# A pre-norm transformer block on one core: the value operands' differences moved into their pair's own iteration, and the background rounding at the end of attention queued behind norms and copies

## The chip, the cores and the metric

The kernel runs on 1 core of one Trainium2 chip. The metric is the device time of one execution in microseconds; before the change it is 2465.94 us, the median of 3 runs (2464.23 to 2466.81). Five engines work side by side, each in the order of its own instruction list: TensorE (PE, matmuls and transpositions through the array), VectorE (DVE), ScalarE (ACT), GpSimd (POOL) and SyncE (SP, which here only issues DMAs). They wait for each other through semaphores.

## The reference

One block with a residual stream of 2048 tokens by 1024 channels, all in float32:

```
x = x + attention(layernorm(x))       # per token: 32 heads of 32 attend to each other
x = x + w3' (silu(w1' xn) * (w2' xn)) # xn = layernorm(x), hidden size 2752
```

Attention is unusual: for each token, the 32 heads' queries (32 x 32) are multiplied with the 32 heads' keys of the same token, a softmax runs over the 32 head scores, and the result weighs the 32 heads' values. So it is 2048 little 32x32 problems, and no token sees another one. The three projections have biases. A fourth projection of the reference ("latent") isn't used for the output.

w1', w2' and w3' are the weights rounded to a 16-level code and back: each block of 64 weights is divided by its largest magnitude, every quotient goes to the nearest of 16 fixed levels, and the result is multiplied by the magnitude again. The kernel must do this rounding itself, with the inputs given in full precision.

## The kernel before

**Products.** Every large product is done by a Strassen-Winograd scheme: operands are cut into four quarters, a few sums and differences of quarters (the names S1 to S4 for the left operand, T1 to T4 for the right one) are made first, and seven products of quarters replace eight. `three`, `fourth` and `differences` (L419 to L430) make S1 to S4 of a token pair's operand with four VectorE operations L420, L421, L422 and L425 of 128x512 each.

**Stages.** Tokens are handled in 16 tiles of 128, in 8 pairs. There are four stages:

1. Query sweep, one iteration per pair (p = 0 to 7). VectorE normalizes the two tiles (L358 writes xn), TensorE transposes xn (L517), four blocks of 512 columns for a pair, and ScalarE copies each block out of PSUM twice: into the operand A in token order (L520) and into the operand V in another token order (L522). The third block's copies go to A21 and V21. PSUM has three buffers `pt` for these blocks. `products` (L373 to L417) multiplies A with the query weights; its helper calls `fill(n)` after some products, and there other work is put in: background turns, and at n = 5 the transpositions of the next pair (`nxt.transposes`). After the products, `nxt.finished()` makes the next pair's A differences and writes A to DRAM (opD), `now.finished_v()` makes the current pair's V differences and writes V (opV). A has two buffers, V, A21 and V21 have one each. `qk_T` turns the query product and stores it; `weight_chunk` makes T1 to T4 of a slice of the key or value weights.
2. Key sweep: A comes back from DRAM, is multiplied with the key weights, and `scores` and `softmax_T` do the 32x32 score problems.
3. Value sweep: V comes back from DRAM and is multiplied with the value weights. `gather` does the 32x32 products of probabilities and values, half a tile per `part()` call, into the one PSUM buffer `at`. After the second half `residual` (L722 to L732) transposes `at` into the tile cx on VectorE (L725), adds it to the tile x1 of the block's input (L729), writes the sum to DRAM (x1d, L731, two DMAs of 128x512) and normalizes it (L358 through `normed`). `keep_T` transposes the normed tile on TensorE (L768), copies it out on ScalarE (L769), makes T1 to T4 on VectorE (L784, tiles xU) and writes all to DRAM.
4. Feed-forward. Weight units of 128 hidden channels (`Unit`, seven products per unit) and then the down projection in groups (`down7`, and `down` at the end). Between the third and the fourth stage, `plain_block` multiplies the first unit (chunk 0) without the seven-product scheme while the last four tiles' `part()` calls and `keep_T` calls are threaded through its steps (L908 to L934).

**The background.** `background` is a generator that rounds the FFN weights, chunk after chunk. One `next` is a turn. A turn is one rounding step: either one VectorE operation (L257, L259, L261), or a ScalarE activation (L266 into a tile sg, two buffers) followed by a VectorE operation (L267); some turns also hold the block maxima (`absmax`, L230 to L238) or the scaling (`scaled`, sixteen ScalarE operations of 128x64 at L218, or one VectorE operation at L214). `advance(n)` takes n turns; `flush` does the transpositions and copies (L178, L179) of a finished chunk. In the feed-forward stage turns are paced by TensorE's time (`spent`).

**What sets the order.** TensorE's instructions are issued as written (`manual_schedule`). For the other engines and the DMA issues a list scheduler sets the order at compile time, from the order in which the program traces them, their dependences and its own estimate of durations; it also hands out the buffers. Three devices steer it. `tc.issue_after(ins)` queues what is traced in the block behind `ins` on `ins`'s engine. `marked(ins)` remembers a ScalarE copy, and where `urgent["rule"]` names "scale" or "step", the background's ScalarE work is queued behind the last remembered copy (`behind`). `held["behind"]`, if set, queues whole background turns behind one VectorE instruction (`turn`); `hook["normed"]` is the newest norm (L358).

Of the kernel before, what the change touches and what calls it, by code (L numbers as in the profile page):

```python
# [14 lines left out]
ALU = mybir.AluOpType  # L15
# [16 lines left out]
TB = 512  # L32
# [37 lines left out]
def preln_block_kernel(  # L70
# [14 lines left out]
    nc = tc.nc  # L85
# [38 lines left out]
    held = {"behind": None}  # L124
# [155 lines left out]
    def advance(n):  # L280
        for _ in range(n):
            with turn():
                next(bg, None)
# [22 lines left out]
    NP = NT // 2  # L306
# [43 lines left out]
    def normed(src, dst, order=None):  # L350
        mv = small.tile([P, 2], FP, tag="mv", name="mv")
        rs = small.tile([P, 1], FP, tag="rs", name="rs")
        mean_var(small, src, mv)
        with tc.issue_after(order["last"]) if order else nullcontext():
            order_end = inv_std(rs, mv[:, 1:2])
        if order is not None:
            order["last"] = order_end.ins
        done = nc.vector.tensor_scalar(dst, src, mv[:, 0:1], rs, ALU.subtract, ALU.mult)  # L358
        hook["normed"] = done.ins
        return dst  # L360
# [185 lines left out]
    nxt = Inputs(0)  # L546
# [25 lines left out]
    opened = last.ins  # L572
# [24 lines left out]
    for p in range(NP):  # L597
        more = p + 1 < NP
        now = nxt
        urgent["rule"] = ("scale",) if p == 0 else ()  # L600
        if more:
            load_x(2 * p + 2)
            load_x(2 * p + 3)
            with nullcontext() if p else tc.issue_after(opened):
                nxt = Inputs(p + 1)
            if p == 0:
                with tc.issue_after(hook["normed"]):
                    nc.vector.tensor_tensor(W["T4"], W["B21"], W["T2"], ALU.subtract)

        def fill(n):  # L610
            if n in (7, 3):
                flush(1)
            if n == 5 and more:
                nxt.transposes(0)
                nxt.transposes(1)
            with nullcontext() if p else tc.issue_after(opened):
                advance({3: 3, 4: 2}.get(n, 0) if p == 0 else int(n != 5))

        cs = products(now.A, fill, (lambda name: None) if more else next_W("k"), ps_t)
        flush(1)  # L620
        if more:
            nxt.finished()
        for j in range(2):
            t = work.tile([P, 32, NH], FP, tag="qd", name="qd", bufs=2)
            qk_T(t, cs[j], qb_sb)
            nc.sync.dma_start(qD[2 * p + j], t)
        with nullcontext() if p else tc.issue_after(opened):
            now.finished_v()
        weight_chunk("kv"[p // 4], p % 4)
        advance(2)  # L630
        if p == NP - 2:
            first = load_A(opD, 0)
# [89 lines left out]
    def residual(i, at, x1):  # L722

        cx = work.tile([P, E], FP, tag="cx", name="cx")
        nc.vector.transpose(  # L725
            cx.rearrange("p (h d) -> p d h", d=D),
            at[:, :, 0:256].rearrange("p c (s d) -> p d s c", d=D),
        )
        nc.vector.tensor_tensor(x1, x1, cx, ALU.add)  # L729
        for n in range(2):  # L730
            nc.sync.dma_start(x1d[i][n], x1[:, ts(n, TB)])  # L731
        return normed(x1, x1)  # L732

    ops = {}

# [51 lines left out]
    for p in range(NP):  # L787
        if p + 1 < NP:
            nextA = load_A(opV, p + 1)
        else:  # L790

            until("2", 0)
            nextA = work.tile([P, 4, 4, P], FP, tag="w0", name="w0")
            nc.sync.dma_start(nextA, wd["2", 0][:, 0:4])
        i = 2 * p - 4

        def fill(n):
            if n in (7, 2, 5, 4) and (p, n) != (1, 7):
                part()
            advance({7: 2, 6: 2, 5: 1, 3: 2}.get(n, 0))  # L800
            if n in (7, 4):
                flush(1)
            if n == 5 and i in x1n:
                keep_T(i, x1n.pop(i))
            if n == 3:
                if p == 0:
                    part()
                elif i + 1 in x1n:
                    keep_T(i + 1, x1n.pop(i + 1))

        cs = products(A, fill, (lambda name: None) if p + 1 < NP else next_op)
        flush(1)
        if p == 0:
            sweep.close()
            sweep = ExitStack()
            work = sweep.enter_context(
                tc.tile_pool(name="workv", bufs=1, side="right", reuse_waits="tile")
            )
        pl = load_tiles(pD, p, "pl", 3)
        for j in range(2):  # L820
            t = work.tile([P, 32, D], FP, tag="vd", name="vd", bufs=3)
            v_T(t, cs[j], vb_sb)
            parts.append(gather(2 * p + j, pl[j], t))
        advance(2)
        A = nextA
    hook["scale"] = "both"
    urgent["rule"] = ()
    left.close()


# [74 lines left out]

    plain = plain_block(A, 0)  # L908
    i = NT - 4
    next(plain)  # L910
    next(plain)
    part()
    advance(1)
    next(plain)
    keep_T(i, x1n.pop(i))
    part()
    advance(2)
    flush()
    next(plain)
    part()  # L920
    advance(2)
    next(plain)
    keep_T(i + 1, x1n.pop(i + 1))
    part()
    advance(3)
    next(plain)
    part()
    advance(3)
    next(plain)
    keep_T(i + 2, x1n.pop(i + 2))  # L930
    hs = {0: next(plain)}
    advance(3)
    held["behind"] = hook["normed"]
    keep_T(i + 3, x1n.pop(i + 3))  # L934
    sweep.close()
    sweep_at.close()
# [20 lines left out]
    class Unit:  # L957
# [13 lines left out]
        def first(self):  # L971
            self.z = ps_z.tile([P, TB], FP, tag="z", name="z")
            self.mul(1, self.z, True, False)
            self.g0 = hp.tile([P, TB], FP, tag="g0", name="g0", bufs=2)
            nc.scalar.copy(self.g0, self.z)  # L975

        def middle(self):
            q = self.q = ps_q.tile([P, TB], FP, tag="q", name="q")
            self.mul(7, q, True, False)
            self.mul(6, self.z, False, False)  # L980
            u2 = self.u2 = hp.tile([P, TB], FP, tag="u2", name="u2")
            nc.scalar.copy(u2, self.z)
            r = ps_r.tile([P, TB], FP, tag="r", name="rr")
            self.mul(2, r, True, True)
            nc.vector.tensor_tensor(self.g0, self.g0, r, ALU.add)  # L985
            nc.scalar.activation(self.g0, self.g0, AF.Silu)
            self.mul(5, self.z, False, False)
            u4 = hp.tile([P, TB], FP, tag="u4", name="u4")
            nc.scalar.copy(u4, self.z)  # L989
            self.h = [new_h(), new_h()]  # L990
            nc.vector.tensor_tensor(self.h[1], u4, q, ALU.add)

# [195 lines left out]
    for n, (g, tbp) in enumerate(passes):  # L1188
        half, sides = None, []
        while now is not None and now.tbp == tbp and now.c in g:  # L1190
            unit = now
            unit.middle()
            if unit.c == min(g[-1], NFULL - 1):
                for c in [c for c in w3T if c not in g]:
                    del w3T[c]
                ask_w3(g)
            if g[-1] == NFULL and unit.c == NFULL - 1:
                half = Half(tbp)
                half.part(0)
                hs[unit.c] = unit.last()  # L1200
                half.part(1)
                hs[NFULL] = half.h
                now = None
            if units:
                now = Unit(*units.pop(0))
                now.first()
            if unit.c < PAIRED and unit.c % 2:
                side = Sides(hs[unit.c - 1], n == 0, len(sides))
                hs[unit.c] = unit.last(side.second)
                sides.append(side.both(hs[unit.c][0]))  # L1210
            elif half is None:
# [46 lines left out]
```

## Time and profile before

| | |
|---|---|
| median of 3 runs | 2465.94 us |
| lowest and highest | 2464.23, 2466.81 us |
| profiled execution, its own time | 2468.05 us |
| its span, first to last instruction | 2466.3 us |
| granted TensorE clock, mean | 0.989 |
| PE, DVE, ACT, POOL busy | 2384.2, 2015.7, 1514.9, 290.0 us |
| DMA | 513.87 MB, mean 208 GB/s |

Busy times are those of instructions of each engine; an engine that waits, or whose sequencer only issues DMAs, counts as idle. In a timeline row the columns are start, length, engine, line, operation, output and inputs by the program's tile names, and the count of merged instructions; a bracket holds the idle time of that engine just before the row, and which engine's instruction ended it. TensorE rows of eight matmuls are one product of the seven (four matmuls of 128x512 in the program, two rows for each in the profile). The stages lie at about 0 to 262 us (queries), 262 to 510 us (keys), 510 to 762 us (values), 762 to 816 us (plain block with the last four tiles), and the rest is the feed-forward.

### The profile page before, as it was taken

To read this page: it belongs to the slowest core of one execution; us is meant where nothing else is said; L and a number is where in the kernel's file an instruction comes from. 1 tells how busy PE (TensorE), PEld (TensorE's weight loads), DVE (VectorE), ACT (ScalarE), POOL (GpSimd) and SP (SyncE) were. 2 spreads that over 40 slices of the span, in tenths; PEclk is the share of its full clock that TensorE was granted. 3 is DMA by queue.
4 is the path that set the end of the run, shared out by engine and by line. 5 is a ranking of instruction groups with operands and counts; after the bars stand their busy time and mean duration, and the time that the engine had idled before them with its cause. 6 is when DMAs were issued, how large, how long until landed. Compare 5 with 4: busy or idle time off the path is not lost.

```text
span 2466.3 us, 36345 instructions
## 1 busy us (share of the span) xinstructions
PE 2384.2 (97%) x14000; PEld 1114.6 (45%) x14000; DVE 2015.7 (82%) x2239; ACT 1514.9 (61%) x2819; POOL 290.0 (12%) x364
## 2 busy tenths in 40 slices
PE   8899999999998899999999999999999999999998
PEld 4444455545554344444444444444444444444433
DVE  8999888679899789898989989899898998861022
ACT  4556644134445678778787786977878778751200
POOL 1010000001001012030030301203012030020300
PEclk9999999999998999999999999999999999999999
DMA  8788643656779577485784858848588385772983
GB/s 320 279 298 351 237 161 115 230 204 224 231 247 317 192 261 164 141 177 187 280 178 141 177 172 298 171 147 182 163 294 194 125 187 160 276 167 78 179 317 113
DMA packets 179549, 513.87 MB, mean 208 GB/s; under 512 B 15984, under 2 KB 70256, under 8 KB 156976
## 3 DMA queue, kind: packets, MB, share of 16 engines
q1 hardware_dynamic: 138672, 438.08, 48.7%
q0 software_dynamic: 40704, 73.47, 18.2%
q8 instruction: 110, 1.80, 0.3%
q14 instruction: 63, 0.52, 0.1%
HBM read 283.69 MB, written 227.80 MB: 207 GB/s over the span
## 4 chain that ended last, share of the span: by engine, by line
DVE 23%; issue 21%; PE 14%; ACT 7%; DMA 3%; POOL 1%; DVEq 0%; POOLq 0%; ACTq 0%; SPq 0%
DVE r L267 15%; PE z L364 5%; DMA x1d<-acc 3%; PE z L1070 2%; ACT sg L266 2%; PE q L364 2%; ACT wn L218 2%; PE po L1151 1%; ACT r L218 1%; PE y L1070 1%; DVE r L259 1%; DVE r L261 1%; ACT acc L1083 1%; DVE am L230 1%; PE rr L364 1%
## 5 line engine op out<-in xcount | busy, mean ns | idle before, releaser
L267 DVE SCALAR_TENSOR_TENSOR r<-sg,r 128x1024 f32<-128x1024 f32 x780 | 946.8, 1214 | 84.8 <-ACT sg L266 51.6
L266 ACT ACTIVATE sg<-wn 128x1024 f32<-128x1024 f32 x780 | 815.1, 1054 | 305.9 <-DVE r L267 280.6
L1085 POOL DMA_DIRECT2D x1d<-acc x280 | 244.2, 926 | 1281.0 <-ACT acc L1083 1238.1
L364 PE MATMUL z<-xB,w 128*128 128x512 f32 x720 | 327.1, 602 | 5.9 <-ACT u L989 4.2
L364 PE MATMUL z<-xT,w 128*128 128x512 f32 x656 | 300.5, 601 | 11.7 <-ACT g L975 8.0
L364 PE MATMUL q<-xT,w 128*128 128x512 f32 x656 | 291.3, 592 | 0.0
L1070 PE MATMUL z<-w,h 128*128 128x512 f32 x496 | 230.8, 593 | 2.9 <-ACT acc L1083 2.9
L364 PEld LDWEIGHTS z<-xB,w 128*128 128x128 f32 x720 | 135.1, 193 | 170.2 <-issue 152.9
L364 PEld LDWEIGHTS z<-xT,w 128*128 128x128 f32 x656 | 123.2, 192 | 165.7 <-issue 139.5
L218 ACT ACTIVATE wn<-wn,rc 128x64 f32<-128x64 f32 x736 | 189.3, 341 | 8.9 <-DVE rc L238 8.9
L364 PEld LDWEIGHTS q<-xT,w 128*128 128x128 f32 x656 | 123.2, 190 | 148.6 <-issue 146.4
L364 PE MATMUL z<-wT,A 128*128 128x512 f32 x384 | 177.1, 604 | 0.1
L364 PE MATMUL q<-wT,A 128*128 128x512 f32 x384 | 172.8, 592 | 0.0
L1070 PE MATMUL y<-w,h 128*128 128x512 f32 x320 | 152.0, 596 | 3.6 <-DVE h L1048 3.1
L364 PE MATMUL z<-wB,A 128*128 128x512 f32 x320 | 148.5, 608 | 2.0 <-ACT u L383 2.0
L364 PE MATMUL rr<-xB,w 128*128 128x512 f32 x328 | 147.5, 592 | 0.0
L1070 PEld LDWEIGHTS z<-w,h 128*128 128x128 f32 x496 | 92.6, 190 | 116.9 <-issue 100.8
L218 ACT ACTIVATE r<-r,am 128x64 f32<-128x64 f32 x456 | 116.6, 344 | 16.1 <-DVE r L267 16.0
L1083 ACT COPY acc<-z 128x512 f32<-128x512 f32 x160 | 92.6, 585 | 38.0 <-PE z L1070 29.7
L364 PEld LDWEIGHTS q<-wT,A 128*128 128x128 f32 x384 | 72.1, 190 | 86.7 <-issue 84.9
L985 DVE TENSOR_TENSOR g<-g,rr 128x512 f32<-128x512 f32 x41 | 28.0, 682 | 100.7 <-PE rr L364 100.7
L137 POOL TENSOR_TENSOR rs<-mv,eps 128x1 f32<-128x1 f32 x32 | 18.0, 562 | 762.5 <-DVE mv L134 762.5
(136 smaller groups left out, 2733.6 us busy)
## 6 DMA issues: line engine op xcount, KB each, us to landing
x1d<-acc POOLq DMA_DIRECT2D x280, 256.0 KB, 6.5
wd<-wop SPq DMA_DIRECT2D x31, 2048.0 KB, 7.3
w<-wd SPq DMA_DIRECT2D x41, 1280.0 KB, 7.7
wn<-in_w_dram SPq DMA_DIRECT2D x63, 512.0 KB, 4.2
xT<-xdT SPq DMA_DIRECT2D x28, 1024.0 KB, 8.5
xB<-xdB SPq DMA_DIRECT2D x24, 1024.0 KB, 7.0
w<-wd SPq DMA_DIRECT2D x42, 512.0 KB, 4.4
w<-wd SPq DMA_DIRECT2D x10, 1536.0 KB, 7.6
```

The lines of the kernel that those rows point to most:

```text
L218: nc.scalar.mul(dst[:, ts(n, BLOCK)], src[:, ts(n, BLOCK)], by[:, n : n + 1])
L230: nc.vector.tensor_reduce(am[:, :nb], v.rearrange("p (b e) -> p b e", e=BLOCK), AX.X, ALU.max, apply_absolute_value=True,)
L259: nc.vector.scalar_tensor_tensor(r, v, edge, r, ALU.is_lt, ALU.max)
L261: nc.vector.scalar_tensor_tensor(r, v, edge, r, ALU.is_gt, ALU.subtract)
L266: nc.scalar.activation(t, v, AF.Copy, bias=-edge * by, scale=by)
L267: nc.vector.scalar_tensor_tensor(r, t, code, r, ALU.min, ALU.max)
L364: nc.tensor.matmul(dst, w[:, k, :], xop[:, k, :], start=start and k == 0, stop=stop and k == 3, skip_group_check=True,)
L985: nc.vector.tensor_tensor(self.g0, self.g0, r, ALU.add)
L1070: nc.tensor.matmul(dst, side[n][:, ts(q, P)], w3T[g[2 * m]][:, W3[n]], start=start and m == 0, stop=stop and m == 1, skip_group_check=True,)
L1083: nc.scalar.copy(t, src)
L1085: nc.gpsimd.dma_start(x1d[8 * tbp + 2 * q + j][n], t, accum_op=ALU.add)
L1151: nc.tensor.matmul(po, hs[c][j][:, ts(q, P)], w3T[c][:, ts(n, 512)], start=(c == g[0]), stop=False, skip_group_check=True,)
```

## The change

It has three parts.

1. Query sweep. `nxt.finished_v()` is called right after `nxt.finished()`: the V differences and the opV write of the next pair are traced in the iteration that transposes this pair, not one iteration later. The first pair's V differences are made at its own `fill(7)`.
2. `residual`. The sum goes into cx and not into x1; the DRAM writes read cx, and the norm reads cx and writes x1. cx has one buffer, x1 three. So the norm no longer overwrites the tile that the writes read, and the next tile's transposition overwrites the one that they read.
3. End of attention. Each of the five `part()` calls inside the plain block is followed by three turns, which are queued behind the newest norm (`last_part`); before, one, two or three turns followed them, and only turns after the last part were queued so. The last pair of the value sweep takes three turns less (no turns at n = 3, one at its end), and the plain block takes three more: 17 and not 14. The rule that queues rounding work on ScalarE behind marked copies stays on until the first seven-product unit of the feed-forward is done, and that unit's copies g0, u2 and u4 are marked.

```diff
         def fill(n):
             if n in (7, 3):
                 flush(1)
+            if n == 7 and p == 0:
+                with tc.issue_after(opened):
+                    now.finished_v()
...
         if more:
             nxt.finished()
+            nxt.finished_v()
...
-        with nullcontext() if p else tc.issue_after(opened):
-            now.finished_v()
...
-        nc.vector.tensor_tensor(x1, x1, cx, ALU.add)
+        nc.vector.tensor_tensor(cx, x1, cx, ALU.add)
         for n in range(2):
-            nc.sync.dma_start(x1d[i][n], x1[:, ts(n, TB)])
-        return normed(x1, x1)
+            nc.sync.dma_start(x1d[i][n], cx[:, ts(n, TB)])
+        return normed(cx, x1)
...
-            advance({7: 2, 6: 2, 5: 1, 3: 2}.get(n, 0))
+            advance({7: 2, 6: 2, 5: 1, 3: 2 if p + 1 < NP else 0}.get(n, 0))
...
-        advance(2)
+        advance(2 if p + 1 < NP else 1)
...
-    urgent["rule"] = ()
...
+    def last_part(turns):
+        part()
+        held["behind"] = hook["normed"]
+        advance(turns)
+
     plain = plain_block(A, 0)
     i = NT - 4
     next(plain)
     next(plain)
-    part()
-    advance(1)
+    last_part(3)
     next(plain)
     keep_T(i, x1n.pop(i))
-    part()
-    advance(2)
+    last_part(3)
     flush()
...
     hs = {0: next(plain)}
-    advance(3)
-    held["behind"] = hook["normed"]
+    advance(2)
     keep_T(i + 3, x1n.pop(i + 3))
...
-            nc.scalar.copy(self.g0, self.z)
+            marked(nc.scalar.copy(self.g0, self.z))
...
-            nc.scalar.copy(u2, self.z)
+            marked(nc.scalar.copy(u2, self.z))
...
-            nc.scalar.copy(u4, self.z)
+            marked(nc.scalar.copy(u4, self.z))
...
             elif half is None:
                 hs[unit.c] = unit.last()
+            urgent["rule"] = ()
```

The changed kernel's lines from L613 on are one to four lines further down, so that `residual`'s transposition is L727 there, its sum L731 and its writes L733.

More of the change, by code (lines that the diff above doesn't have):

```diff
@@ L911, in preln_block_kernel @@
     next(plain)
-    part()
-    advance(1)
+    last_part(3)
     next(plain)
     keep_T(i, x1n.pop(i))
-    part()
-    advance(2)
+    last_part(3)
     flush()
     next(plain)
-    part()
-    advance(2)
+    last_part(3)
     next(plain)
     keep_T(i + 1, x1n.pop(i + 1))
-    part()
-    advance(3)
+    last_part(3)
     next(plain)
-    part()
-    advance(3)
+    last_part(3)
     next(plain)
@@ L931, in preln_block_kernel @@
     hs = {0: next(plain)}
-    advance(3)
-    held["behind"] = hook["normed"]
+    advance(2)
     keep_T(i + 3, x1n.pop(i + 3))
```

## Prediction

> **What bounds the kernel now.** I read the page first, then busy time by stretch, then TensorE's own idle time in order, then what VectorE and ScalarE did in those moments.
>
> ```profile
> span 2466.3 us, 36345 instructions
> PE 2384.2 (97%) x14000; PEld 1114.6 (45%) x14000; DVE 2015.7 (82%) x2239; ACT 1514.9 (61%) x2819; POOL 290.0 (12%) x364
> ```
>
> TensorE works 97% of the span, and neither its instructions nor their order differ between the two builds. The change can only remove idle TensorE time, at most 2466.3 - 2384.2 = 82.1 us, and the time lost at a lower clock. Busy time by stretch (columns: stretch, its length, then busy us of PE, PEld, DVE, ACT, POOL, then granted clock) shows where it lies:
>
> ```profile
> 0.00:250.00 250.00, 228.57 (x633) 110.45 (x634) 231.56 (x310) 134.50 (x281) 24.64 (x52) 0.97 0.83 313
> 250.00:500.00 250.00, 245.62 (x4050) 130.46 (x4049) 199.17 (x203) 102.56 (x205) 0.00 (x0) 1.00 0.50 188
> ...
> 750.00:850.00 100.00, 81.28 (x1003) 42.08 (x1003) 82.13 (x93) 58.54 (x127) 5.45 (x8) 0.88 0.71 239
> 850.00:1650.00 800.00, 786.23 (x1986) 352.56 (x1985) 732.29 (x788) 631.80 (x1135) 122.63 (x140) 1.00 0.68 195
> ```
>
> The query sweep (0 to 262 us) and the end of attention (750 to 850 us) hold nearly all that an ordering change can reach. The feed-forward half idles 13.8 us in 800. In TensorE's timeline the bracket is the idle time before a row and its releaser. Query sweep:
>
> ```profile
> 62.82 0.66 PE L517 MATMUL pt<-ident,xn 128*128 128x128 f32 x4 [2.06 <-ACT V L522]
> 63.32 5.30 PE L364 MATMUL y<-wB,A 128*128 128x512 f32 x8
> ...
> 92.92 0.66 PE L517 MATMUL pt<-ident,xn 128*128 128x128 f32 x4 [2.39 <-ACT V L522]
> 93.41 3.60 PE L364 MATMUL y<-wB,A 128*128 128x512 f32 x8
> ```
>
> The fourth transposition of each pair waits for ScalarE to empty a PSUM buffer (seven such waits, 12.95 us in all). End of attention:
>
> ```profile
> 781.56 1.54 PE L464 MATMUL cx<-vd,pl 32*32 32x32 f32 x128 [6.85 <-DVE cx L725]
> 783.03 5.86 PE L364 MATMUL z<-xB,w 128*128 128x512 f32 x8
> ...
> 798.87 0.33 PE L464 MATMUL cx<-vd,pl 32*32 32x32 f32 x8 [3.10 <-issue]
> 799.13 6.35 PE L364 MATMUL z<-xB,w 128*128 128x512 f32 x8
> ...
> 815.02 1.06 PE L768 MATMUL pt<-ident,x 128*128 128x128 f32 x8 [0.39 <-DVE x L358]
> ...
> 830.95 5.80 PE L364 MATMUL z<-xT,w 128*128 128x512 f32 x8 [8.00 <-ACT g L975]
> ```
>
> That is 6.85 + 3.10 + 0.39 + 8.00 = 18.3 us of waiting, and the three products of eight rows after the long waits took 5.86, 6.35 and 5.80 us where another one takes 3.60: another 7.2 us at a lower clock, 25.5 in all. VectorE shows why the first wait is there: cx could be read at 770.2 us, when the context matmuls ended, and its transposition L725 came at 779.6, behind rounding steps.
>
> ```profile
> 776.74 1.22 DVE L259 SCALAR_TENSOR_TENSOR r<-wn,r 128x1024 f32<-128x1024 f32 x1
> ...
> 778.48 1.22 DVE L261 SCALAR_TENSOR_TENSOR r<-wn,r 128x1024 f32<-128x1024 f32 x1
> 779.61 1.90 DVE L725 STREAM_TRANSPOSE cx<-cx 128x1024 f32<-128x1024 f32 x1
> ```
>
> **Part 1, value differences.** Nothing is added: per pair the same four DVE operations (0.60 us apart each) and one opV write (0.33 us of issue). What moves is their place, and with it the copies. Before, V's single buffer was held by the pair before until its differences and write were done, so ScalarE copied A, A, A21, V21 first and freed the first PSUM buffer with the fourth copy after u4. In the compiled order of the changed kernel it copies A, V, A, V, ..., so the second copy frees one: 2 x 0.49 = 0.98 us less wait for each of six pairs, 5.9 us; the first pair keeps its 1.33 us, since its V copies still stand behind the A copies for the opV write. A21 is copied 0.98 us later; its difference L420 ran at 62.63 and the T3 product that needs S3 at about 75.3, so that is free. From below: VectorE was busy 164.1 of the 172.1 us between 63.3 and 235.4, and 4.05 of its 8.0 idle us are waits for the norm's POOL step, which stay. Following its new order with these durations, the second norm of the third pair ends about 120.9 us against TensorE's arrival at 114.5: a new wait of 6.4 us that eats most of what the first pairs won; from there on I find TensorE 4 to 5.5 us ahead of before. I take 5; ends 0 (VectorE binds) and 16.8 (12.95 us of waits, and 1.70 + 2.16 us of low-clock products at 63.32 and 124.30). SP: in two pairs the second xt load now stands behind four weight writes of some 0.6 us each; the load lands in 5.9 us and its statistics may wait 2 us. I take 0, since VectorE is late there too, and keep the 2 for the range.
>
> **Part 2, residual out of place.** The same four DVE operations and two writes per tile. L358 no longer waits for x1d<-x to be read (7.0 us in two waits before), but cx has one buffer, so the next tile's transposition L725 waits for this tile's write. That write lands in 2.0 / 2.8 / 8.8 us (min, median, max), and tiles come some 13 us apart in the value sweep; cover 13 - 3.2 (transposition, sum) - 8.8 = 1 us at worst. Queued behind a late transposition would be the tile's sum, statistics and norm, the steps that now follow the norm, and TensorE's next context, which needs the PSUM that the transposition reads. At 753.46, the one long wait, the transposition then starts 1.3 us earlier than the 754.78 of before. I take 0; ends -7 and +6 (one landing at the maximum, uncovered).
>
> **Part 3, turns behind the norms, copies marked.** The background turns are as many (9 + 14 before, 6 + 17 after). Steps traced after a part now stand behind the newest norm on VectorE, and on ScalarE behind the newest marked copy. I followed the four engines' new orders from 744 us on with the durations above (1.13 to 1.24 us a step, 1.98 a transposition, 1.2 a sum, 1.28 statistics, about 1 for POOL, 0.8 a norm, 3.43 a product, 1.29 half a context). Tile 13's transposition runs 771.0 to 773.0, held by xU writes (4.3 us to land) and no longer by steps, and TensorE reaches the next context at 774.6: 6.85 us of wait gone. Tile 14's runs 785.5 to 787.4 against an arrival at 785.0: a wait of 2.4. The last norm ends near 806.5 against 801.3: 5.2. Copy g0 stands behind sg steps that are done by 812.3, and TensorE needs it at 814.4: the 8.00 us wait is gone. What is late next is VectorE: u2 stands behind three steps and comes at 823.9 for 821.7 (2.2), u4 at 834.4 for 831.2 (3.2). New waits 13.0. One low-clock product after the 5.2 us wait costs 2.5 (mean of 2.26, 2.75, 2.20 is 2.4); those after the shorter ones I take as hidden in the u2 and u4 waits, which VectorE sets. 25.5 - 13.0 - 2.5 = 10. Ends: 3 (all four waits followed by a low-clock product, 9.6) and 25.5. Marking Unit's copies costs no instruction; the steps behind them run on an engine that is 61% busy.
>
> Behind this, TensorE's gain must survive: VectorE ends the same steps only 848 - 842 = 6 us sooner, so it enters the feed-forward 4 to 7 us later against TensorE. It idles 67.7 us of the next 800, so I take 0; ends 0 and 4 given back.
>
> On the clock, rows first: 2.06 us of waiting was followed by a low-clock product (5.30), 2.39 us was not (3.60), 3.10 was (6.35). The Trainium skill, "TensorE: Matmul & The Clock Gate", section "Part 1: The HAM clock gate", says that the clock halves after a wholly idle window of about 3.4 us. By that rule the query sweep's waits cost no clock and no low-clock product could be won there: its top end would be 12.95 instead of 16.8. The trace speaks against it as a threshold on the wait's length, and my sum claims no clock in that sweep either way.
>
> **Sum.** -5 + 0 - 10 = -15 us. The profiled execution took 2468.05 us (span 2466.3 and 1.75 around it), 2.1 above the median of 2465.94. So 2453 for it, 2451 for the median.
>
> **Rivals.**
> All of it: VectorE uses its whole 8 us of idle time in the query sweep (with the second pair's 1.0, 9 us) and the end's new waits halve with no low-clock product (25.5 - 6.5 = 19): 2438. For: PSUM and ScalarE have room. Against: VectorE is 93 to 100% busy there.
> VectorE sets the pace: query sweep 0, the end only the 6 us that VectorE gains: 2460. For: VectorE at 98 to 100% from 155 to 211 us.
> No reach: the waits only change their names, as cx's write takes the place of the norm's and u2/u4 that of g0: 2466, within 1.
> Slower: the norm comes late. V's four operations now stand ahead of the query transpositions and so of the next pair's statistics and norm; if that makes TensorE wait 2.4 us (4 x 0.60) more before the transpositions of seven pairs, each with a low-clock product like that at 63.32 (1.70), it costs 28.7 us, less the end's 10: 2485. It decides from 10 / 7 = 1.4 us a pair on. For: the third pair's 6.4 us. Against: per iteration the count of VectorE's operations is as before, and in my count the other pairs' norms are on time.
>
> **Numbers.** My forecast 0.56, all of it 0.12, VectorE's pace 0.16, no reach 0.08, slower 0.08. A measurement here can tell about 0.2%, 5 us, from no change. Faster: 0.56 + 0.12 + 0.12 of the third; same: the other 0.04 and 0.08; slower 0.08. Range 2440 to 2466: past the second rival to the middle of the no-reach case, and down to the upper third of the first; outside lie 0.08, 0.04 and 0.08, 0.20 in all.
>
> **What would show it.** Right: V's waits at L517 fall from 2.1-2.4 to about 1 us; no wait for cx before the context near 775 us and none for g0 near 820; TensorE's idle time in the first 250 us falls by about 5 and between 745 and 845 by about 5, with fewer low-clock products; the feed-forward as long as before. Wrong: new waits of transpositions for xn L358 beyond the third pair, waits of cx L727 for x1d above 5 us, or a longer stretch from unit 1 to the end, with ScalarE's copies late behind steps.

## The result and the profile after

The changed kernel takes 2478.01 us, the median of six runs (2475.36 to 2478.57), against 2465.73 us for six runs of the kernel before: a ratio of 1.0047, 95% interval 1.0036 to 1.0058. It is 12 us slower, where 15 us less were forecast. The profiled execution is the lowest of its six (2475.36 us) and that of before lies 2.3 us above its median, so the two traces differ by 7.3 us of span and show that much of the 12.3. First the page of the changed kernel:

```profile
span 2473.6 us, 36349 instructions
PE 2385.5 (96%) x14000; PEld 1115.8 (45%) x14000; DVE 2018.1 (82%) x2239; ACT 1510.0 (61%) x2819; POOL 286.0 (12%) x364
```

TensorE's work is the same within 1.3 us. By stretch (columns as for the kernel before):

```profile
0.00:250.00 250.00, 227.94 (x628) 110.35 (x629) 230.33 (x307) 137.53 (x297) 23.32 (x52) 0.97 0.82 311
250.00:500.00 250.00, 239.91 (x3907) 127.04 (x3906) 193.10 (x199) 98.13 (x190) 0.00 (x0) 0.98 0.47 176
500.00:750.00 250.00, 238.81 (x4113) 124.89 (x4112) 216.80 (x227) 108.64 (x224) 12.86 (x22) 0.99 0.65 223
750.00:850.00 100.00, 90.25 (x1365) 47.95 (x1364) 83.74 (x93) 46.78 (x87) 5.22 (x10) 0.93 0.81 271
850.00:1650.00 800.00, 781.91 (x1979) 351.13 (x1978) 736.63 (x796) 640.97 (x1175) 123.00 (x140) 1.00 0.68 194
```

The end of attention is better filled (90.25 us of TensorE in 100, before 81.28, though the later start puts a little more of the value sweep into the window). The query sweep isn't, and the stretch from 250 to 500 us, which the forecast left alone, lost 5.7 us of TensorE time.

TensorE's order is the same in both kernels, so the k-th matmul of one trace is the k-th of the other, and the difference of their starts is the lag at that point (positive: the changed kernel is behind):

| matmul | before, us | after, us | lag, us |
|---|---|---|---|
| product y in the iteration p = 2 (query sweep) | 93.41 | 90.20 | -3.2 |
| product y near the end of the query sweep | 213.07 | 214.35 | +1.3 |
| first scores of the key sweep | 276.38 | 283.91 | +7.5 |
| inside the product behind them | 280.75 | 290.69 | +9.9 |
| first weight transposition after 620 us (value sweep) | 627.44 | 637.29 | +9.9 |
| near the end of the value sweep | 752.63 | 771.64 | +19.0 |
| first unit, product with T2 | 830.95 | 838.80 | +7.9 |
| first unit, product with B22 | 847.77 | 856.26 | +8.5 |
| last matmul | | | +7.3 |

So in these two traces the change gained nothing in the query sweep, lost 8.6 us at the first scores and 9.1 us in the value sweep, won 10.5 us at the end of attention, and 1.2 us more behind it. Two or three microseconds of such a lag can be the scatter of single traces: ten of the runs below leave the query sweep as it was, and against the same trace of before they stand at -2.3 to +0.2 us at the matmul of 93.41 and at +0.8 to +3.4 at that of 213.07. TensorE's timeline has the places. Query sweep and first scores (the bracket is the idle time ahead, with its releaser):

```profile
60.74 1.24 PE L517 MATMUL pt<-ident,xn 128*128 128x128 f32 x8 [0.28 <-DVE xn L358]
...
89.71 0.66 PE L517 MATMUL pt<-ident,xn 128*128 128x128 f32 x4 [0.29 <-ACT AV L522]
...
123.32 1.97 PE L517 MATMUL pt<-ident,xn 128*128 128x128 f32 x8 [7.17 <-DVE xn L358]
...
210.95 0.66 PE L517 MATMUL pt<-ident,xn 128*128 128x128 f32 x4 [2.75 <-ACT AV L522]
...
283.91 1.77 PE L450 MATMUL sc<-kd,ql 32*32 32x32 f32 x128 [5.93 <-DMA ql<-qD]
285.61 6.10 PE L364 MATMUL z<-wT,A 128*128 128x512 f32 x8
```

The waits for V's copies did shrink, but the late norm in the iteration p = 3 (the prediction's "third pair") takes 7.17 us. At 283.91 the scores wait for the query tile ql; before, they started behind a product without a wait:

```profile
272.84 3.60 PE L364 MATMUL q<-wT,A 128*128 128x512 f32 x8
276.37 1.77 PE L450 MATMUL sc<-kd,ql 32*32 32x32 f32 x128
```

The end of attention in the changed kernel:

```profile
794.16 1.29 PE L464 MATMUL cx<-vd,pl 32*32 32x32 f32 x128 [0.46 <-DVE cx L727]
...
807.24 0.98 PE L770 MATMUL pt<-ident,x 128*128 128x128 f32 x7 [2.29 <-issue]
...
829.35 1.54 PE L770 MATMUL pt<-ident,x 128*128 128x128 f32 x8 [2.92 <-DVE x L358]
...
856.26 5.40 PE L364 MATMUL z<-xB,w 128*128 128x512 f32 x8 [2.68 <-ACT u L989]
```

The 6.85 us for cx and the 8.00 us for g0 are gone; waits of 2 to 3 us for a norm and for a unit copy stand in their place.

Three theories were made of this. **Theory A**, two separate losses: SyncE's queue holds up the query loads (part 1), and the freed norm runs too early on VectorE (part 2). SyncE's rows show the first. In the changed kernel the writes of the last slice of value weights (wtDv) wait for VectorE, and the loads A and ql stand behind them:

```profile
250.85 1.17 SPq L580 DMA_DIRECT2D cB<-in_wvT_dram  x2
252.08 0.74 SPq L594 DMA_DIRECT2D A<-opD  x1
270.19 0.33 SPq L587 DMA_DIRECT2D wtDv<-cB  x1
...
273.54 0.38 SPq L594 DMA_DIRECT2D A<-opD  x1
273.97 1.64 SPq L693 DMA_DIRECT2D ql<-qD  x3
```

```profile
SPq L587 <- DVE cB L583: 17.3, 1, 17.3
```

The second fence is SyncE's waits between 240 and 290 us: 17.3 us for the chunk's second subtraction. In the kernel before the same queue went on:

```profile
249.55 0.38 SPq L534 DMA_DIRECT2D opV<-AV  x1
249.99 2.05 SPq L587 DMA_DIRECT2D wtDv<-cB  x2
...
257.81 0.84 SPq L691 DMA_DIRECT2D ql<-qD  x2
```

There all four loads of the chunk had gone out at 212 us and its subtractions had been done by 230, in the query sweep; with part 1 its last two loads (cB) go out only at 250.85, behind the stores of qd, and its subtractions run at 267.7 to 273.1 us. The first ql load is issued 16 us later than before. The Trainium skill, "DMA: Bandwidth & Descriptors", section "Anatomy of one DMA — SWDGE (gpsimd) path", says that any wait on a semaphore takes place on the issuing sequencer, ahead of dispatch; the 17.3 us row, with the later loads behind it, agrees.

For part 2, VectorE's rows in the value sweep of the changed kernel:

```profile
631.71 0.21 DVE L134 BATCH_NORM_AGGREGATE mv<-st 128x2 f32<-128x12 f32 x1
632.85 0.81 DVE L358 TENSOR_SCALAR x<-cx,mv,rs 128x1024 f32<-128x1024 f32 x1 [0.93 <-POOL rs L138]
633.58 1.95 DVE L439 STREAM_TRANSPOSE vd<-ce 128x1024 f32<-128x1024 f32 x1
635.45 1.17 DVE L267 SCALAR_TENSOR_TENSOR r<-sg,r 128x1024 f32<-128x1024 f32 x1
```

and at the same place of the kernel before:

```profile
623.60 0.21 DVE L134 BATCH_NORM_AGGREGATE mv<-st 128x2 f32<-128x12 f32 x1
623.73 1.94 DVE L439 STREAM_TRANSPOSE vd<-ce 128x1024 f32<-128x1024 f32 x1
625.55 1.21 DVE L267 SCALAR_TENSOR_TENSOR r<-sg,r 128x1024 f32<-128x1024 f32 x1
...
628.38 0.83 DVE L358 TENSOR_SCALAR x<-x,mv,rs 128x1024 f32<-128x1024 f32 x1
```

Before, the norm had to wait for the write of the sum, and the scheduler put four instructions ahead of it; by then GpSimd's rs was done. Now nothing but rs holds it, it stands first, waits 0.93 us with VectorE idle, and what TensorE needs soon (the values vd, the rounding step that ScalarE's scaling and then the weight transposition follow) comes later: from mv to the end of that step it is 3.16 us before and 4.91 after. Nobody reads the normed tile until the next iteration. TensorE's row for the weight transposition that follows, before and then in the changed kernel:

```profile
627.43 0.33 PE L178 MATMUL ptw<-ident,r 128*128 128x128 f32 x1 [0.36 <-ACT r L218]
```

```profile
637.29 0.81 PE L178 MATMUL ptw<-ident,r 128*128 128x128 f32 x2 [2.15 <-ACT r L218]
```

Later in the sweep the changed kernel has waits of 0.79 to 1.35 us for cx, ce and co (at 691.58, 724.66, 733.21 and 747.81), where the rows of before show no wait of TensorE between 632 and 745 us.

**Theory B**, one loss: the value sweep only passes on the key sweep's delay through the background. **Theory C**, slack: the 10 us at the end of attention only take up lateness, so nothing was won there.

### The profile page after: what moved, and what is told of

It is laid out like the page before. It is cut to its first block, busy times and chain, and to the rows that moved or that the text cites. A ratio compares the mean times of both kernels' runs of the same rounds, so it can differ in the third digit from the quotient of the medians.

```text
span 2473.6 us, 36349 instructions
## 1 busy us (share of the span) xinstructions
PE 2385.5 (96%) x14000; PEld 1115.8 (45%) x14000; DVE 2018.1 (82%) x2239; ACT 1510.0 (61%) x2819; POOL 286.0 (12%) x364
## 4 chain that ended last, share of the span: by engine, by line
DVE 23%; issue 21%; PE 14%; ACT 7%; DMA 3%; POOL 1%; DVEq 0%; SPq 0%; ACTq 0%; POOLq 0%
DVE r L267 15%; PE z L364 5%; DMA x1d<-acc 3%; PE z L1070 2%; ACT sg L266 2%; PE q L364 2%; ACT r L218 1%; ACT wn L218 1%; PE po L1151 1%; ACT acc L1083 1%; DVE r L259 1%; PE y L1070 1%; DVE r L261 1%; DVE am L230 1%; PE rr L364 1%
## 5 line engine op out<-in xcount | busy, mean ns | idle before, releaser
L364 PEld LDWEIGHTS z<-wT,A 128*128 128x128 f32 x384 | 71.2, 192 | 80.6 <-issue 77.5
```

The lines of the kernel that those rows point to most:

```text
L364: nc.tensor.matmul(dst, w[:, k, :], xop[:, k, :], start=start and k == 0, stop=stop and k == 3, skip_group_check=True,)
```

## The experiments

**Each part alone, and the change without part 1.** The edits are the change's own: the first three kernels are the kernel before with one part each, and the fourth is the changed kernel with part 1 undone, by this edit:

```diff
-            if n == 7 and p == 0:
-                with tc.issue_after(opened):
-                    now.finished_v()
...
-            nxt.finished_v()
...
+        with nullcontext() if p else tc.issue_after(opened):
+            now.finished_v()
```

> The kernel before with the first part of the change alone: the V differences of the next pair in the pair's own iteration. Theory (two losses, one gain): the query sweep ends at about 262 us as before, and the first scores of the key sweep then wait some 6 us for ql<-qD, because SyncE's queue holds the writes of the last weight chunk ahead of the ready loads; with the low-clock product behind it this costs 8 to 10 us, and nothing is lost in the value sweep: 2474 us (2472 to 2477). Rival 'one cause for both losses': the value sweep's loss is the key sweep's delay passed on by VectorE's background work, so this run loses in both places: 2483 us. Rival 'taken up': the end of attention waited for weights and norms anyway and takes up what comes late before it, so this run ends at 2466 us although the scores wait. My own forecast of this part was a gain of 5 us: 2461 us.

> The kernel before with the second part alone: the residual sum goes to the context's tile, the writes read it there, and the norm goes from there to the residual's tile. Theory: the norm L358 now stands on VectorE where it has to wait for GpSimd's rs (7.6 us in 10 waits between 600 and 790 us in the changed kernel, 1.2 in 2 before), and the next transposition of a context waits for the write of x1 out of the one tile; VectorE has no spare time in the value sweep, so the plain block begins 7 to 9 us later: 2474 us (2471 to 2476), with nothing lost at the start of the key sweep. Rival 'one cause for both losses': without the key sweep's delay nothing is lost here: 2466 us. My forecast had this part at 0 as well.

> The kernel before with the third part alone: seventeen turns of weight work in place of fourteen at the end of attention, held behind the newest norm, the last value pair with six turns, and the later end of the rule. Theory: the gain of the end of attention stands by itself: 2455 us (2453 to 2458), with the wait of 8.0 us for ScalarE's g0 gone. Rival 'taken up': the 10 us by which the changed kernel's lag falls there are only a delay that found slack; then this run is at 2466 us, within 3. Rival 'needs the second part': the turns end behind the norms only with the norm's own tile free; then it gains 3 to 5 us: 2462 us.

> The changed kernel with the first part undone. Theory: the loss of the key sweep (8 to 10 us) goes and the other two parts stay: 2466 + 8 - 10 = 2464 us, up to 2468; the first ql<-qD is issued at about 258 us and the first scores wait for nothing long. Rival 'one cause for both losses': both losses go and the gain of the end stays: 2456 us. Rival 'taken up': about 2466 us, with no lag at the plain block and no gain at the end.

Measured, all against 2465.62 us for the kernel before on the same chip:

| kernel | median, us | ratio, 95% interval |
|---|---|---|
| part 1 alone | 2475.69 | 1.0042 (1.0029 to 1.0054) |
| part 2 alone | 2472.79 | 1.0026 (1.0017 to 1.0035) |
| part 3 alone | 2463.49 | 0.9988 (0.9979 to 0.9997) |
| parts 2 and 3 | 2468.85 | 1.0011 (1.0002 to 1.0020) |

Part 1 costs 10.1 us and part 2 costs 7.2, each without the other, so B falls. In the trace of part 1 alone the lag goes from 2.6 to 7.5 us at the first scores and to 8.5 in the product behind them, and grows to 12.5 by the end of the value sweep, where no one step stands out; in that of part 2 alone it is at most 0.5 from the first scores until 540 us, and 9 at 760. C isn't settled by part 3's time: it gives 2.1 us, far less than the 8 to 13 expected, and C had allowed for 3. In its trace the lag goes from +2.8 to -4.4 us over the end of attention, that of part 2 alone from 9.2 to 6.2. But not all of such a gain is the change's: part 1 alone leaves the order of VectorE and ScalarE there as it was, and its trace goes from 12.5 to 9.3; in part 1 with other query loads (below), which has the same orders there, it goes from 1.5 to -2.6. So some 3 to 4 of the 10.5 us can be lateness that was taken up, or the one trace of before. A net gain, which lateness that is taken up can't give, is shown by two runs further down, with ratios of 0.9984 (0.9976 to 0.9993) and 0.9968; as the whole explanation C falls with them. The three medians add up to 10.1 + 7.2 - 2.1 = 15.2 us, the whole change has 12.3. Parts 2 and 3 together came out at +3.2, a little above the range of theory A (2464 to 2468 us).

Why part 3 alone is weak shows in VectorE's rows at the start of the plain block:

```profile
779.53 0.21 DVE L134 BATCH_NORM_AGGREGATE mv<-st 128x2 f32<-128x12 f32 x1
786.24 0.81 DVE L358 TENSOR_SCALAR x<-x,mv,rs 128x1024 f32<-128x1024 f32 x1 [6.51 <-DMA x1d<-x]
```

The turns are held behind the newest norm, this norm waits for the write of its tile, and so VectorE stands for 6.5 us. That led to the next run.

**Part 3 with the free norm for the last four tiles only.**

```diff
+        s = cx if i >= NT - 4 else x1
-        nc.vector.tensor_tensor(x1, x1, cx, ALU.add)
+        nc.vector.tensor_tensor(s, x1, cx, ALU.add)
...
-        return normed(x1, x1)
+        return normed(s, x1)
```

> The third part with the second part's free norm for the last four tiles alone; the other tiles' norms stay in place as in the kernel before, and the first part is left out. Theory: the third part alone gained 2 us because its turns are held behind the newest norm, and that norm waits 6.5 us for the write x1d<-x (VectorE and ScalarE stand from 780 to 786 us); with the free norm the wait goes, and the value sweep keeps its pace since its norms stay in place: 2457 us (2454 to 2460). Rival 'the end is VectorE's': the turns are VectorE's work, which has to be done in any order, so it stays near 2463 us.

2463.53 us, ratio 0.9990 (0.9982 to 0.9998): the forecast was missed. The 6.5 us wait is gone (0.93 is left at 781.74), but the total is that of part 3 alone. TensorE's rows show waits that took its place:

```profile
790.27 1.03 PE L769 MATMUL pt<-ident,x 128*128 128x128 f32 x8 [1.84 <-ACT sg L266]
...
812.95 1.94 PE L769 MATMUL pt<-ident,x 128*128 128x128 f32 x8 [5.35 <-DVE x L358]
...
840.36 5.40 PE L364 MATMUL z<-xB,w 128*128 128x512 f32 x8 [2.57 <-ACT u L988]
```

The last norm is 5.35 us late. VectorE was busy only 9.97 of the 15 us from 765 to 780 (14.85 in the kernel before): with the turns held, nothing filled its wait for a write out of xU, and the turns came afterwards, ahead of that norm.

```profile
775.46 0.69 DVE L785 TENSOR_TENSOR xU<-xT,xU 128x512 f32<-128x512 f32 x1 [4.08 <-DMA xdT<-xU]
```

**Part 1 with the first query loads on another queue.** Only these two loads leave SyncE's queue; the order of everything else on it stays.

```diff
-            nc.sync.dma_start(t, src[2 * p + j])
+            queue = nc.gpsimd if src is qD and p == 0 else nc.sync
+            queue.dma_start(t, src[2 * p + j])
```

> The first part alone, with the first pair's two query loads of the key sweep issued from GpSimd's queue, where nothing stands ahead of them; SyncE's queue keeps the weight chunk's writes. Theory (SyncE's order is the whole of the 7 us step at the first scores): the scores begin at about 276 to 278 us, and the kernel is back at 2467 us (2465 to 2470) from 2476. Rival 'VectorE': the first keys kd are late by themselves, since the chunk's four subtractions stand on VectorE at 268 to 274 us among the keys' own; then the step stays at 3 us or more and the kernel at 2470 to 2474. Rival 'memory': the loads take 9 us to land beside the other traffic whenever they start; then 2472 us or more.

2466.43 us against 2466.43: ratio 1.000 (0.999 to 1.001). The scores start with no wait, though the wtDv writes still go out at 270 us and the chunk's subtractions still stand among the keys' work. TensorE's row, then GpSimd's:

```profile
277.87 1.79 PE L450 MATMUL sc<-kd,ql 32*32 32x32 f32 x128
```

```profile
228.89 1.13 POOL L694 DMA_DIRECT2D ql<-qD  x2 [29.91 <-DVE r L267]
```

The two loads go out 29 us earlier than in the kernel before, but there the scores had no wait either. So the loads' place in SyncE's queue was the whole loss of part 1, within the interval of about 2.5 us either way, and what the moved differences gain by themselves is nothing that can be told: in this trace TensorE is 3.3 us ahead at 93 us and 0.9 us behind at 213.

**Part 2 with its norms later.** The first attempt traced the norm (all tiles but the last four) at the next part of attention; the second also held that of a pair's first tile behind the values' bias, where the kernel before has it.

```diff
+        if isinstance(order, int):
+            held_norms[order].append(apply)
...
     def part():
+        if held_norms[0]:
+            held_norms[0].pop()()
...
-            v_T(t, cs[j], vb_sb)
+            biased = v_T(t, cs[j], vb_sb)
+            if held_norms[1]:
+                with tc.issue_after(biased.ins):
+                    held_norms[1].pop()()
```

> The second part alone, with the norms of all tiles but the last four traced at the next part of attention, so that most of them stand one or two VectorE instructions later. Theory (VectorE's wait for GpSimd's rs ahead of the norm, 8.4 us in 11 waits of the value sweep against 2.6 in 4, is most of the loss): the waits fall to 3 to 5 us and the kernel gains 3 to 5 us on the second part alone: 2469 us (2467 to 2471). Rival 'one tile': the loss comes from the one context tile, whose writes the next transposition must wait for, and from the transfers; then it stays at 2472 to 2473 us.

> The second part alone, with the norms of the value sweep held where the kernel before has them: that of a pair's first tile behind the bias of the pair's values, that of its second behind the next part of attention. Only the tiles differ from the kernel before: the sum and the writes use the one context tile. Theory (the loss of the second part is the norm's place: with its own source it goes ahead of the values' transposition, where it waits 0.9 us for GpSimd's rs and holds up the values and the weight work that TensorE waits for): the lag at the plain block falls from 9 to 0 to 3 us and the kernel to 2467 us (2465 to 2469). Rival 'one tile' (the next transposition of a context waits for the writes out of the one tile, and the transfers shift): 2471 to 2473 us as with the norm left early.

The first gave 2472.86 us (1.0026, 1.0016 to 1.0037) for a forecast of 2469, no better than part 2 as it was, and taken alone it spoke for the rival. In its compiled order the norm of the pair's first tile still stood straight behind mv; tracing it later didn't move it (why not isn't shown; perhaps VectorE looked free there to the scheduler). VectorE's waits for rs between 590 and 765 us fell from 7.0 us in 9 to 4.5 in 5, so VectorE's idle time for GpSimd is not the price, or not most of it. The second run gave 2462.28 us against 2466.88: ratio 0.9981 (0.9972 to 0.9990), better than its forecast (2465 to 2469). The same stretch of VectorE (lines are shifted: L360 is the norm, L448 the values' transposition, L451 their bias, L424 co):

```profile
625.75 0.21 DVE L134 BATCH_NORM_AGGREGATE mv<-st 128x2 f32<-128x12 f32 x1
625.88 1.94 DVE L448 STREAM_TRANSPOSE vd<-ce 128x1024 f32<-128x1024 f32 x1
...
629.42 1.21 DVE L451 TENSOR_TENSOR vd<-vd,vb 128x1024 f32<-128x1024 f32 x1
...
631.76 0.80 DVE L360 TENSOR_SCALAR x<-cx,mv,rs 128x1024 f32<-128x1024 f32 x1
```

TensorE's wait for the weight transposition is short again:

```profile
629.57 0.80 PE L178 MATMUL ptw<-ident,r 128*128 128x128 f32 x2 [0.35 <-ACT r L218]
```

The lag at the end of the value sweep is 1.8 us and not 9, while the one context tile, its writes and its transposition are those of part 2. VectorE's order isn't quite that of before (a few neighbours of the norms change places), but the rival, the one tile, is ruled out. So the norm's place was the loss, and with it put right part 2 is a gain of 4.6 us. Where it is made isn't shown: its trace wins 5.0 us in the plain block, but the run with the query loads elsewhere, which has the orders of before there, wins 4.1.

**All three parts, mended.** Part 1 with the query loads on GpSimd's queue, the free norm for the last four tiles, part 3 as it is.

```diff
+        s = cx if i >= NT - 4 else x1
...
+            queue = nc.gpsimd if src is qD and p == 0 else nc.sync
```

> All of the change, with the free norm for the last four tiles alone and the first pair's query loads on GpSimd's queue. Theory: the first part neither gains nor loses once the query loads stand free, since what the query sweep wins until 93 us is lost again to the late second norm of the third pair: as the third part with four free norms, 2457 us, within 2 either way. My forecast's view of the first part (a gain of 5 us): 2452 us. If the first part costs in other places too: 2460 us or more.

2462.74 us, ratio 0.9984 (0.9976 to 0.9993). That is within 1 us of the run without part 1 beside it (2463.53), so part 1 is worth nothing here; the level of 2457 us was missed, with the same waits as above (3.02 us for the last norm, 2.92 for a unit copy).

**The turns and the hold of part 3**, both with the free norms for the last four tiles. First the turns as before (nine in the last value pair, then 1, 2, 2, 3, 3, 3), with the hold; then seventeen turns without it:

```diff
-    last_part(3)
+    last_part(1)
...
-        held["behind"] = hook["normed"]
         advance(turns)
```

> The third part with free norms for the last four tiles, and with the turns given out as in the kernel before: nine in the last value pair and 1, 2, 2, 3, 3, 3 behind it; the hold behind the newest norm, the marks and the rule stay. Theory (the three turns moved out of the last value pair leave VectorE 6 us idle between 765 and 780 us and make the last norm 5.4 us late at 813): that wait falls under 2 us and the kernel gains 3 to 4 us on the third part: 2460 us (2457 to 2462). Rival 'the hold' (the turns' place behind the norms is what keeps VectorE idle, however many they are): it stays at 2463 to 2465 us.

> The third part with free norms for the last four tiles, its seventeen turns not held behind the newest norms: the hold begins where the kernel before has it, behind the last turn. Theory: the turns fill VectorE's idle time from 765 to 786 us, so the last norm is no longer 5.4 us late; 2460 us (2457 to 2462). Rival 'the copies': without the hold the norms and copies stand behind the turns as before, the 8 us wait for ScalarE's g0 stays away because of the marks alone, and 6 to 7 us of waits for norms come back: 2465 us or more.

Against 2466.88 us: 2462.13 (0.9981, 0.9972 to 0.9991) and 2460.40 (0.9968, 0.9959 to 0.9978). The second interval lies clear of that with the hold (0.9982 to 0.9998): holding the turns cost 0.9990 - 0.9968 = 0.0022, about 5 us by the ratios and 3.6 by the medians. The first doesn't, though its wait for the last norm is gone as forecast, so whether the turns' distribution matters isn't settled. Without the hold the wait for the last norm is 3.25 us, and the wait for g0 doesn't come back:

```profile
814.84 1.94 PE L769 MATMUL pt<-ident,x 128*128 128x128 f32 x8 [3.25 <-DVE x L358]
...
839.72 3.70 PE L364 MATMUL z<-xB,w 128*128 128x512 f32 x8 [0.68 <-ACT u L988]
```

**Held norms with the marks, with and without the new turns.** Two runs on the kernel with part 2's norms held behind the values; the first adds only the marks and the later end of the rule, the second also the seventeen turns, not held.

```diff
-            nc.scalar.copy(self.g0, self.z)
+            marked(nc.scalar.copy(self.g0, self.z))
```

> The second part with its norms held (as in the run before that reached 2462 us), plus the marks and the later end of the rule from the third part; the turns stand in number and place as in the kernel before. Theory 'marks' (of the third part it is the marks that take away the 8 to 9 us wait for ScalarE's copy of g0, and the turns' new places only trade waits): that wait goes, about 2.5 to 3 us of it come back as a wait for the u copies at the next product, and with the 4.6 us of the held norms the kernel comes to 2457 us (2455 to 2460). Rival 'turns' (the turns' places are needed too): 2461 to 2462 us, with a wait of 3 us or more for a norm or a copy left before the first unit.

> The same with the seventeen turns of the third part in place of fourteen and six in the last value pair, none of them held behind the newest norm. Theory 'marks': the turns only trade waits, so it is within 2 us of the run with the turns as before, 2457 us. Rival 'turns': it is 3 us or more faster than that run, at 2457 against 2461 us.

2460.31 us (0.9973, 0.9962 to 0.9983) and 2458.97 us (0.9966, 0.9954 to 0.9978), against 2466.57. Held norms without the marks had shown this wait for g0, first fence; with the marks the longest wait of that unit is the second (TensorE in both):

```profile
827.21 6.35 PE L373 MATMUL z<-xT,w 128*128 128x512 f32 x8 [9.00 <-ACT g L989]
```

```profile
839.22 3.70 PE L373 MATMUL z<-xB,w 128*128 128x512 f32 x8 [1.07 <-ACT u L1002]
```

The marks, with the later end of the rule, take the wait away without any change of the turns. What that is worth in time isn't shown: the interval overlaps that of held norms without them (0.9972 to 0.9990), and 2460.31 us lies just above the forecast of 2455 to 2460. The two runs' intervals overlap as well, so with a difference of 1.3 us between the medians nothing was shown for the turns' new places. The last run is the best of the study: 7.6 us faster than the kernel before, where the change as it was made is 12.3 us slower.

## Why the prediction was wrong

- **Query sweep, "I take 5".** The waits for V's copies fell from 12.95 to 6.62 us, a gain of 6.3 as forecast (5.9). The late norm of the "third pair" came as forecast too (7.17 for 6.4; at this place before already had a norm wait of 2.07, at 121.43, which the sum doesn't mention), but two more waits for norms, 0.28 and 1.67 us, stand beside it, and the step "from there on I find TensorE 4 to 5.5 us ahead of before" failed: TensorE is 1.3 us behind at 213 us. All waits for copies and norms come to 15.0 us before and 15.7 after, the time lost in low-clock products to 3.9 and 4.2: VectorE takes back what ScalarE's copies give. The lower end, 0, was the right value.
- **SyncE, "I take 0".** This is the first step that sank the sum. The queue was looked through for the second xt load of two pairs, not for what stands behind the last weight chunk, whose last loads slid to the end of the query sweep and its subtractions into the key sweep. Price: 8.6 us in the trace, 9 to 10 us by the medians of part 1 alone and of part 1 with the loads elsewhere (10.1 and 0.0 us above the kernel before that ran beside each).
- **Part 2, "I take 0; ends -7 and +6".** The second. The bounds were worked out for the wait of the next transposition on the write out of cx, and that was 2.7 us, once. The price lay in the other direction: a norm that waits for less moves forward in VectorE's order, ahead of work that is needed sooner. It is 7.2 us over the whole kernel for part 2 alone, and 9.1 in the value sweep of the changed kernel.
- **Part 3, "25.5 - 13.0 - 2.5 = 10".** Right for the stage in the changed kernel: waits of 10.3 us (0.46, 0.74, 2.29, 0.47, 0.76, 2.92 and 2.68) and three low-clock products of 6.20, 4.85 and 5.40 us for 3.60, 5.7 us more, make 25.5 - 16.0 = 9.5. That the total fits is partly luck, since the waits are 2.7 us less than counted and the low clock took 3.2 more. And it had been read off the order of the whole change and against one trace of before: the third part alone is worth 2.1, and 3 to 4 us of the difference come in that stretch without any change there.
- **Feed-forward, "I take 0".** Right: the lag goes from 8.5 to 7.3 us.
- The first two signs listed as "wrong" didn't appear: there was no norm wait later than the "third pair" and no wait of cx for x1d above 5 us. The list named no sign for either loss. Of the signs for "right", the two long waits at the end went, but TensorE's idle time in the first 250 us didn't fall (22.1 us, before 21.4). The rival on the slower side had the right sign and the wrong place: a norm too late in the query sweep was priced at 28.7 us, and what happened in the value sweep was a norm too early.

The terms as they came out in the trace: +1.3 + 8.6 + 9.1 - 10.5 - 1.2 = 7.3, for -5 + 0 + 0 - 10 + 0.

## What to carry to other kernels

Freeing an instruction from a wait is also a change of order: a list scheduler starts it as soon as it can, and on a busy engine that puts it ahead of work with nearer consumers, so give it an order when you take its dependence away. When a step moves, read the in-order DMA queue to its end, past the stage's border, and ask of each waiting issue which ready loads stand behind it. And before holding background work behind a milestone, look at what the engine waits for until then, for the work can no longer fill that time: here it was 6.51 us for the milestone itself and, with that wait gone, 4.08 us for a write ahead of it; without the hold the kernel was 4 to 5 us faster.

## What the runs showed that was not expected

A query load is issued at 273.97 us and the scores can start at 283.91, 9.9 us later, though it carries 0.5 MB; the traces put the landing of the first four of these loads at 3.3 to 11.4 us (median 10.2) in the changed kernel, and 3.3 to 9.9 (8.6) in the kernel before. So a load issued 16 us late cost 6 to 8 us only because before, by these times, it had landed some 9 us ahead of its use.

A wait that was followed by a low-clock product was as short as 2.68 us: the row at 856.26 has products on both sides, its own took 5.40 us for 3.60, and the granted clock from 856.3 to 861.4 us was 0.67. In the query sweep the waits of 1.92 us (153.28, with 5.29 us for the product behind it) and 2.75 us (210.95, then 5.30) stand among transpositions, so that 3.72 and 4.55 us passed without a product. The longest of that sweep, 7.17 us, was followed by a product of 4.37 us: the granted clock was 0.50 from 119.8 us on, during the wait, and 1.00 again from 126.7. In this kernel the length of a wait alone doesn't tell what the next product costs. The Trainium skill, "TensorE: Matmul & The Clock Gate", section "Part 1: The HAM clock gate", gives an idle window of about 3.4 us as the condition; the 2.68 us here are shorter, and the measurement decides.
